# A two-layer graph network on one core: layer 1's leaky step moved from VectorE to GpSimd, and a mask made earlier

## The chip, the cores and the metric

The kernel runs on one core of one Trainium2 chip. The engines are TensorE (PE in the profile, PEld for its weight loads), VectorE (DVE), ScalarE (ACT), GpSimd (POOL) and SyncE (SP, which here only issues DMAs). Each engine works through its own instructions in the order in which they were written, and waits on semaphores for the others. The metric is the device time of one execution in microseconds.

## The reference

There are 16 graphs of 1024 nodes with 256 features, and an adjacency matrix of 0 and 1 for each. Layer 0 is attention with 8 heads over the neighbours, layer 1 attention with scores of its own and a leaky step. Each layer works on `h = relu(layernorm(x))` and adds its result to `x`.

```python
# layer 0: Q, K, V = proj(Wq, bq), proj(Wk, bk), proj(Wv, bv), 8 heads of 32
scores = einsum('bhnd,bhmd->bhnm', Q, K) * SCALE
scores = where(adj == 0, -inf, scores)
out    = einsum('bhnm,bhmd->bhnd', softmax(scores), V)
x      = x + einsum('bno,po->bnp', out, Wo) + bo
# layer 1, h = relu(layernorm(x))
e_k    = leaky_relu(einsum('bid,bjd->bij', h * a_k[:, 0], h), negative_slope=0.2)   # k = 0..3
scores = where(adj == 1, e_0, -9e15)      # and e_1, e_2, e_3 where adj is 2, 3, 4
x      = x + einsum('bij,bjd->bid', softmax(scores), h)
```

With an adjacency of 0 and 1 alone only `e_0` counts. The kernel checks this while it runs, and has a slow path (`layer_1_of_kinds`) for other values, which these inputs do not enter.

## The kernel before, in words

Work goes in tiles of 128 rows: 8 tiles (`NT`) to a graph, 128 in all. The main loop has 129 steps `s`, and in each step several tiles at different stages are worked on at once:

- `now` (`Attend`): layer 0's attention of tile `s`. For each head h, `scores` (L435, PE) writes 128x1024 scores into PSUM, `softmax_max` (L447, DVE) scales them, adds the mask and finds the row's extreme, `softmax_exp` (L455, ACT) takes the exponential one head later, and two heads later the result is transposed: heads 0, 1, 4 and 5 by DVE in blocks (L376) and four DMAs (L381), heads 2, 3, 6 and 7 by PE (L555) and copies on ACT (L556). `combine` (L490, PE) multiplies by the values.
- `was` (`Attend`): the end of tile `s - 1`: reciprocals of the sums (L471 and L472 on DVE, `wide` L474 on POOL, recT L484 on ACT), output matmul (L505), `residual` (L511, DVE), `norms` (statistics L188 and L189 on DVE, then `norm_of`, a chain of about 18 very small POOL instructions, L162 to L178), `normed` (L523, ACT). `gone` is the same tile one step later still: `turn_normed` (L530, PE) and the copy L534 (ACT).
- `nxt` (`Attend`): preparation of tile `s + 1`: `load_queries` (L402, a DMA from SP), `flag` (L427, ACT: reads the adjacency tile, leaves in `kinds_seen` whether it holds other values than 0 and 1) and `mask` (L415, POOL: writes -1e30 where the adjacency is 0, as bf16, over the same buffer `neg`). There are ten `neg` buffers, since layer 1 reads a mask again nine steps later. The adjacency tile (L406, a DMA from POOL) has one buffer.
- `edge` (`Edges`): layer 1 of tile `s - 9`, which is one graph and a tile later. `prepare` (L577, POOL) multiplies by a_0 into `ha`, `score` (L587, PE) makes the scores in two halves, `softmax_max` (L601, DVE) negates, masks and finds the row's extreme `top`, `leak` applies the leaky step, `softmax_exp` (L613, ACT) takes the exponential. In the next step the tile is `edge_was`: transposed in blocks by DVE, `gather` (L631, PE), `store` (L640, DVE, and a DMA).
- `piece`, `piece_was`, `piece_nxt`: the rows of the next graph are normalised and projected to queries, keys and values, one tile a step; keys are written to memory twice (L321, from SP and from POOL) and loaded as eight key tiles of a graph (`load_key`, L356, from POOL) around a change of graph, at the places in `KEY_STEPS`.

The order is written out by hand (`manual_schedule`): eight places h = 0 to 7 in a step, each with a list of calls. Before the change, `flag` and `mask` stand at h = 3 behind `load_queries`, `edge.softmax_max` at h = 2, `edge.leak` at h = 4, `edge_nxt.prepare` and the adjacency load at h = 4, `norms` at h = 5, `edge.softmax_exp` at h = 6, `was.normed` at h = 7. The exponential of head h - 1 stands at h, so that of head 7 comes first in the next step.

The tiles of the last graph (`last`, 8 of 128) go through layer 1 after the main loop, in a short loop of their own.

Of the kernel before, what the change touches and what calls it, by code (L numbers as in the profile page):

```python
# [8 lines left out]
F32 = mybir.dt.float32  # L9
# [5 lines left out]
ALU = mybir.AluOpType  # L15
AX = mybir.AxisListType

P = 128
# [5 lines left out]
SLOPE = 0.2  # L24
# [18 lines left out]
def gnn_kernel(  # L43
# [18 lines left out]
    nc = tc.nc  # L62
    B, N, D = x.shape
# [15 lines left out]
    work = ctx.enter_context(tc.tile_pool(name="work", bufs=2))  # L79
    ptp = ctx.enter_context(tc.tile_pool(name="ptp", bufs=7))  # L80
    dram = ctx.enter_context(tc.tile_pool(name="dram", bufs=2, space=bass.MemoryType.DRAM))
    small = ctx.enter_context(tc.tile_pool(name="small", bufs=4))
# [111 lines left out]
    class Piece:  # L194
# [5 lines left out]
        def __init__(self, b, first, n=1):  # L200
            self.b, self.first, self.n = b, first, n
            self.cols = slice(first * P, (first + n) * P)
            self.projected, self.halved, self.again, self.queries = [], [], [], []
            self.tags = ("xin", "h0", "hT", "halves", "hTm") if n == 1 else ("pT", "pT", "qt", "p", "blocks")
# [182 lines left out]
    h1s, h1Ts, x1ds, masks = {}, {}, {}, {}  # L387
# [171 lines left out]
    class Edges:  # L559


        def __init__(self, b, t, last=False):
            self.b, self.t = b, t
            self.rows = slice(t * P, (t + 1) * P)
            self.side = sides[t % 2 if last else 1]
            self.tags = {"sel": ("p", 4), "pT1": ("pT", 7)} if last else {}
            if last and t % 2:
                self.tags |= {"ha": ("hT", 1), "x1b": ("x1", 1)}
# [28 lines left out]

        def softmax_max(self):
            self.sel = self.buffer("sel", [P, N])
            top = small.tile([P, 1], F32, tag="top")  # L600
            nc.vector.tensor_tensor_reduce(  # L601
                out=self.sel, in0=self.e, in1=masks[self.b, self.t], scale=-1.0, scalar=3e38,
                op0=ALU.add, op1=ALU.min, accum_out=top,
            )
            self.nmx = small.tile([P, 1], F32, tag="nmx1")
            nc.vector.scalar_tensor_tensor(self.nmx, top, SLOPE, top, ALU.mult, ALU.min)

        def leak(self):
            nc.vector.scalar_tensor_tensor(self.sel, self.sel, SLOPE, self.sel, ALU.mult, ALU.min)

        def softmax_exp(self):
            self.total = small.tile([P, 1], F32, tag="total")
# [97 lines left out]
    def attend_of(s):  # L710
        return Attend(*divmod(s, NT)) if 0 <= s < B * NT else None
# [9 lines left out]
    with tc.manual_schedule():  # L721
        first = [Piece(0, 0, 4), Piece(0, 4, 4)]
        piece_was, piece_next = Piece(1, 0), piece_of(0)
        now, nxt = attend_of(0), attend_of(1)
# [36 lines left out]
        piece, edge, edge_was = piece_next, None, None  # L761
# [8 lines left out]
        for s in range(B * NT + 1):  # L770
            b, t = divmod(s, NT)

            def load_keys(h, end):
                if t == NT - 1 and b + 1 < B and 2 * h + end in KEY_STEPS:
                    load_key(b + 1, KEY_STEPS.index(2 * h + end))
                if t == 0 and 0 < b < B and 2 * (HEADS + h) + end in KEY_STEPS:
                    load_key(b, KEY_STEPS.index(2 * (HEADS + h) + end))

            nxt2, edge_nxt, piece_nxt = attend_of(s + 2), edges_of(s + 1), piece_of(s + 1)
            for h in range(HEADS):  # L780
                ending, eh = (now, h - 1) if h >= 1 else (was, HEADS - 1)
                turning, th = (now, h - 2) if h >= 2 else (was, HEADS + h - 2)

                load_keys(h, 0)


                if now:
                    now.scores(h)
                if h == 0 and piece_was:
                    piece_was.split()  # L790
                if h == 1 and piece_was:
                    piece_was.split()
                if h == 2 and edge:
                    edge.softmax_max()
                if h == 5:
                    if was:
                        was.residual()
                    norms(was, piece_nxt)
                if h == 6 and edge_was:
                    edge_was.gather(1)  # L800
                if h == 6 and piece_was:
                    piece_was.split()
                    piece_was.split()
                    piece_was.write_queries()
                if now:
                    now.softmax_max(h)
                if h == 6 and edge_was:
                    edge_was.store()
                if h == 4 and edge:
                    edge.leak()  # L810


                if ending:
                    ending.softmax_exp(eh)

                if h == 1 and gone:
                    gone.turned_normed()


                if h == 3:  # L820
                    if piece_was:
                        piece_was.project(1, 0)
                        piece_was.project(1, 1)
                    if was:
                        was.combine(1)
                    if piece_was:
                        piece_was.biased()
                    if was:
                        was.combined()
                if turning and th in BY_BLOCKS:  # L830
                    turning.turn_blocks(th)
                    turning.place_blocks(th)
                elif turning:
                    turning.turn(th, 0)
                    turning.turn(th, 1)


                if h == 0:
                    if piece_was:
                        piece_was.write_again()  # L840
                    if edge:
                        edge.score(0)
                    if gone:
                        gone.turn_normed()
                    if edge_was:
                        edge_was.turn_blocks()
                        edge_was.place_blocks()
                if h == 1:
                    if edge:
                        edge.score(1)  # L850
                    if was:
                        was.reciprocals()
                    if piece_nxt:
                        piece_nxt.load()
                    if piece_was:
                        piece_was.write_again()
                if h == 2:
                    if piece_was:
                        piece_was.values()
                    if was:  # L860
                        was.turn_reciprocals()
                        was.turned_reciprocals()
                        was.add_bias()
                    if edge_was:
                        edge_was.load_nodes()
                if h == 3:
                    if nxt:
                        nxt.load_queries()
                        nxt.flag()
                        nxt.mask()  # L870
                if h == 4:
                    if was:
                        was.output()
                    if piece:
                        piece.normed()
                    if edge_nxt:
                        edge_nxt.prepare()
                    if nxt2:
                        nxt2.load()
                if h == 5:  # L880
                    if edge_was:
                        edge_was.gather(0)
                    if piece:
                        piece.turn()
                    if piece_was:
                        piece_was.high()
                        piece_was.high()
                    if piece:
                        piece.turned()
                if h == 6:  # L890
                    if edge:
                        edge.softmax_exp()
                    if was:
                        was.keep()
                    if now:
                        now.load_nodes()
                    if piece:
                        piece.project(0, 0)
                        piece.project(0, 1)
                if h == 7:  # L900
                    if now:
                        now.combine(0)
                    if piece:
                        piece.high()
                        piece.high()
                    if was:
                        was.normed()
                load_keys(h, 1)
            gone, was, now, nxt = was, now, nxt, nxt2
            edge_was, edge = edge, edge_nxt  # L910
            piece_was, piece = piece, piece_nxt
# [6 lines left out]
        for i in range(1, len(tiles) + 2):  # L918
            edge = tiles[i] if i < len(tiles) else None
# [30 lines left out]
        top = small.tile([1, B + 1], F32, tag="tops", bufs=1)  # L950
# [41 lines left out]
```

## Time and profile before

| | |
|---|---|
| median of 3 runs | 3208.38 us (3190.67, 3208.38, 3210.05) |
| the profiled execution, first to last instruction | 3197.8 us |
| PE, DVE, ACT, POOL busy | 95%, 87%, 77%, 54% |
| granted clock of TensorE, mean | 0.985 |
| mask L415 on POOL, 128x1024 | 128 times, 3.647 us each |
| leaky step L609 on DVE, 128x1024 | 120 times, 1.216 us each (and 8 in the last graph) |

The profiled execution is one of its own; the span from its first to its last instruction is the only time that it shows, and it lies 10.6 us below the median of the runs. A row of the groups in the profile names line, engine, operation, the tiles written and read with their shapes, the count, then the busy time in us and the mean of one instruction in ns, and behind the second bar the idle time of the engine just before these instructions with what ended it. A row of the timeline names start and length in us, engine, line and operation; in square brackets stands how long the engine had been idle, and who released it.

### The profile page before, as it was taken

The page shows a single profiled execution, that of the slowest core. Times are in us where ns is not written, and L with a number is a line of the kernel's source. Part 1 is how long each engine was busy: PE and PEld are TensorE (multiplying, and loading weights), DVE is VectorE, ACT ScalarE, POOL GpSimd, SP SyncE. Part 2 cuts the span into 40 slices and gives each one's busy share as a digit, 9 for nine tenths or more (in the row PEclk, how much of TensorE's full clock was granted, in tenths as well). Part 3 has the DMA queues.
Part 4 walks back from the last instruction along what each step waited for, and adds up shares of the span by engine and source line. Part 5 has one row for each costly group of instructions (what it writes and reads, how often), then busy time and mean ns, then how long its engine had stood idle before and what let it go on. Part 6 is the DMA issues. An engine that isn't in the chain of part 4 may idle for free. (4 is left out here: it accounts for less than half of the span.)

```text
span 3197.8 us, 97634 instructions
## 1 busy us (share of the span) xinstructions
PE 3033.3 (95%) x36018; PEld 2216.3 (69%) x36018; DVE 2797.9 (87%) x5111; ACT 2454.3 (77%) x4829; POOL 1728.1 (54%) x3883
## 2 busy tenths in 40 slices
PE   5889999999999999999999999999999999998998
PEld 3667767777677777777677777777767677776663
DVE  3888989899898998989899998998989889898984
ACT  3887878788787877878788787887878778787761
POOL 2555555555555555555555655555555655555541
PEclk8999999999999999999999999999999999999999
DMA  6787788887888788788887878788887878888653
GB/s 226 219 244 233 227 273 233 259 240 231 270 240 272 226 253 249 226 277 234 252 238 230 275 233 273 230 254 263 235 272 226 269 228 232 267 240 249 194 161 91
DMA packets 747156, 762.90 MB, mean 239 GB/s; under 512 B 71281, under 2 KB 692209, under 8 KB 746673
## 3 DMA queue, kind: packets, MB, share of 16 engines
q1 hardware_dynamic: 678432, 542.34, 58.3%
q0 software_dynamic: 65040, 210.03, 20.3%
q8 instruction: 290, 4.75, 0.6%
q10 hardware_dynamic: 3200, 4.19, 0.4%
q14 instruction: 194, 1.58, 0.1%
HBM read 252.98 MB, written 167.77 MB: 132 GB/s over the span
## 5 line engine op out<-in xcount | busy, mean ns | idle before, releaser
L455 ACT ACTIVATE p<-p,nmx 128x1024 f32<-128x1024 f32 x1024 | 1178.5, 1151 | 249.6 <-DVE nmx L447 248.9
L447 DVE CUSTOM_DVE_ANT_0 p<-s,neg 128x1024 f32<-128x1024 f32 x1024 | 1233.3, 1205 | 92.0 <-issue 49.8
L435 PE MATMUL s<-k,qt 128*128 128x512 f32 x2048 | 795.0, 469 | 77.6 <-DMA qt<-qd 57.4
L415 POOL TENSOR_SCALAR neg<-adj 128x1024 bf16<-128x1024 int32 x128 | 466.8, 3647 | 411.8 <-ACT neg L427 411.8
L376 DVE STREAM_TRANSPOSE blocks<-p 128x1024 f32<-128x1024 f32 x520 | 642.3, 1235 | 11.3 <-ACT p L613 10.8
L556 ACT COPY pT<-trp 128x512 f32<-128x512 f32 x1024 | 543.6, 581 | 86.5 <-PE trp L555 78.6
L490 PE MATMUL acc<-pT,v 128*32 128x128 f32 x16384 | 525.1, 277 | 25.7 <-DMA pT<-blocks 24.3
L555 PE MATMUL trp<-ident,p 128*128 128x128 f32 x4096 | 534.7, 274 | 0.1
L555 PEld LDWEIGHTS trp<-ident,p 128*128 128x128 f32 x4096 | 480.9, 141 | 72.5 <-ACT pT L556 3.0
L490 PEld LDWEIGHTS acc<-pT,v 128*32 128x32 f32 x16384 | 450.7, 111 | 97.6 <-DVE ot L640 41.2
L631 PE MATMUL acc<-h,pT 128*32 128x256 f32 x8192 | 495.8, 383 | 4.0 <-DVE ot L640 3.2
L435 PEld LDWEIGHTS s<-k,qt 128*128 128x128 f32 x2048 | 330.3, 192 | 210.2 <-issue 122.6
L587 PE MATMUL s<-h1T,ha 128*128 128x512 f32 x992 | 471.1, 598 | 0.0
L631 PEld LDWEIGHTS acc<-h,pT 128*32 128x32 f32 x8192 | 242.6, 110 | 208.4 <-issue 58.7
L474 POOL COPY wide<-rec 128x256 f32<-128x256 f32 x128 | 50.8, 397 | 491.4 <-DVE rec L472 491.4
L321 POOL DMA_DIRECT2D kd<-halves x240 | 168.8, 703 | 228.7 <-DVE halves L294 216.2
L601 DVE CUSTOM_DVE_ANT_0 sel<-s,neg 128x1024 f32<-128x1024 f32 x120 | 147.0, 1225 | 126.4 <-PE s L587 126.4
L587 PEld LDWEIGHTS s<-h1T,ha 128*128 128x128 f32 x992 | 171.5, 193 | 124.1 <-issue 124.1
L455 ACT ACTIVATION_READ_ACCUMULATOR p<-p,nmx 128x1 f32 x1024 | 193.4, 189 | 0.0
L484 ACT COPY recT<-acc 128x256 f32<-128x256 f32 x128 | 47.8, 373 | 177.3 <-PE acc L480 177.3
L273 PEld LDWEIGHTS acc<-hT,wkT 128*128 128x128 f32 x960 | 120.8, 197 | 76.7 <-issue 47.3
L273 PE MATMUL acc<-hT,wkT 128*128 128x128 f32 x960 | 144.3, 295 | 27.3 <-DVE halves L294 26.1
(126 smaller groups left out, 4025.1 us busy)
## 6 DMA issues: line engine op xcount, KB each, us to landing
pT<-blocks SPq DMA_DIRECT2D x2560, 128.0 KB, 3.1
qt<-qd SPq DMA_DIRECT2D x128, 512.0 KB, 5.9
adj<-in_adj POOLq DMA_DIRECT2D x127, 512.0 KB, 5.5
qd<-halves SPq DMA_DIRECT2D x240, 256.0 KB, 4.6
k<-kd POOLq DMA_DIRECT2D x120, 512.0 KB, 6.8
kd<-halves POOLq DMA_DIRECT2D x240, 128.0 KB, 3.4
kd<-halves SPq DMA_DIRECT2D x240, 128.0 KB, 3.2
xb<-in_x POOLq DMA_DIRECT2D x128, 128.0 KB, 3.4
```

Source lines behind the costliest of these rows:

```text
L273: nc.tensor.matmul(ps, lhsT=wT[:, fc, oc * P : (oc + 1) * P], rhs=(self.hT, self.hTm)[which][:, fc, :], start=(fc == 0), stop=(fc == NC - 1),)
L321: queue.dma_start(out=kds[self.b][oc, :, :, twice, self.cols], in_=halves.rearrange("p (w n) -> p w n", w=2),)
L376: nc.vector.transpose(blocks.rearrange("p b j q -> p j b q"), p)
L415: nc.gpsimd.tensor_scalar(self.neg, self.adj, 0.0, MASKED, ALU.is_equal, ALU.mult)
L435: nc.tensor.matmul(self.ps[:, cols], lhsT=self.qt[:, h, :], rhs=keysets[self.b][h][:, cols], start=True, stop=True,)
L447: nc.vector.tensor_tensor_reduce(out=p, in0=sides[h in (3, 5, 7)], in1=self.neg, scale=-SCALE, scalar=FLOOR, op0=ALU.add, op1=ALU.min, acc ...
L455: nc.scalar.activation(p, p, AF.Exp, bias=nmx, scale=-1.0, accum_out=self.sums[:, h : h + 1])
L490: nc.tensor.matmul(sums_place[r * HD : (r + 1) * HD, g * P : (g + 1) * P], lhsT=vs[self.b][:, j, place_of(h) : place_of(h) + HD], rhs=self ...
L555: nc.tensor.transpose(tr[:, j, :], p[:, jj * P : (jj + 1) * P], ident)
L556: copy(pT[:, half * 4 : half * 4 + 4, :], tr)
L587: nc.tensor.matmul(self.e[:, cols], lhsT=self.ha[:, c, :], rhs=h1Ts[self.b][:, c, cols], start=(c == 0), stop=(c == NC - 1),)
L631: nc.tensor.matmul(sums_place[a * HD : (a + 1) * HD, :], lhsT=self.pT[:, j, a], rhs=h1s[self.b][:, j, :], start=(j == 0), stop=(j == NT - 1),)
```

## The change

The leaky step of layer 1's negated scores is `min(y, 0.2 y)`. Before, DVE does it in one instruction for a tile (and one small one for the row's extreme). After, `softmax_max` scales the scores by 0.2 as it negates them, so that the leaky step becomes `min(y, 5 y) = y + 4 min(y, 0)`; for all tiles but the last graph's, POOL computes it in four parts of 256 columns, each with a `tensor_scalar` (min with 0, times 4) into a small buffer `less` and an addition; the row's extreme is treated in the same way by two small POOL instructions. The last graph's tiles keep both instructions on DVE. `leak` goes from h = 4, behind the head's `softmax_max`, to the end of h = 3. `flag` and `mask` of the next tile go from h = 3 to the beginning of the list at h = 2.

```diff
-            self.b, self.t = b, t
+            self.b, self.t, self.last = b, t, last
...
         def softmax_max(self):
             self.sel = self.buffer("sel", [P, N])
-            top = small.tile([P, 1], F32, tag="top")
+            self.top = small.tile([P, 1], F32, tag="top")
             nc.vector.tensor_tensor_reduce(
-                out=self.sel, in0=self.e, in1=masks[self.b, self.t], scale=-1.0, scalar=3e38,
-                op0=ALU.add, op1=ALU.min, accum_out=top,
-            )
+                out=self.sel, in0=self.e, in1=masks[self.b, self.t], scale=-SLOPE, scalar=3e38,
+                op0=ALU.add, op1=ALU.min, accum_out=self.top,
+            )
+
+        def leak(self):
+            if self.last:
+                self.nmx = small.tile([P, 1], F32, tag="nmx1")
+                for to, y in ((self.nmx, self.top), (self.sel, self.sel)):
+                    nc.vector.scalar_tensor_tensor(to, y, 1 / SLOPE, y, ALU.mult, ALU.min)
+                return
+            g = nc.gpsimd
+            less = small.tile([P, 1], F32, tag="less1")
+            g.tensor_scalar(less, self.top, 0.0, 1 / SLOPE - 1, ALU.min, ALU.mult)
             self.nmx = small.tile([P, 1], F32, tag="nmx1")
-            nc.vector.scalar_tensor_tensor(self.nmx, top, SLOPE, top, ALU.mult, ALU.min)
-
-        def leak(self):
-            nc.vector.scalar_tensor_tensor(self.sel, self.sel, SLOPE, self.sel, ALU.mult, ALU.min)
+            g.tensor_tensor(self.nmx, self.top, less, ALU.add)
+            part = N // 4
+            for i in range(4):
+                sel = self.sel[:, i * part : (i + 1) * part]
+                less = work.tile([P, part], F32, tag="less", bufs=1)
+                g.tensor_scalar(less, sel, 0.0, 1 / SLOPE - 1, ALU.min, ALU.mult)
+                g.tensor_tensor(sel, sel, less, ALU.add)
...
-                if h == 4 and edge:
-                    edge.leak()
...
                 if h == 2:
+                    if nxt:
+                        nxt.flag()
+                        nxt.mask()
                     if piece_was:
                         piece_was.values()
...
                 if h == 3:
                     if nxt:
                         nxt.load_queries()
-                        nxt.flag()
-                        nxt.mask()
+                    if edge:
+                        edge.leak()
```

## The prediction

> **What bounds the kernel now.** I read first the page's busy times, then the waits, then one ordinary step as a timeline.
>
> ```profile
> PE 3033.3 (95%) x36018; PEld 2216.3 (69%) x36018; DVE 2797.9 (87%) x5111; ACT 2454.3 (77%) x4829; POOL 1728.1 (54%) x3883
> ```
>
> PE is nearly full and POOL is half idle. One ordinary step, mask to mask (length, then busy time of PE, PEld, DVE, ACT, POOL), shows PE without a gap:
>
> ```profile
> 1064.56:1087.78 23.22, 23.22 (x284) 17.13 (x283) 21.73 (x42) 19.22 (x39) 12.96 (x30) 1.00 0.81 230
> ```
>
> The starts of the mask (L415) give the step: 272.92 us to 2909.37 us is 110 steps of 24.0 us; ordinary ones take 23.2, the two around a change of graph about 26, and the last seven (to 3068.1) 22.7. What POOL's idle half consists of stands in the waits from 400 to 3000 us (total, times, longest):
>
> ```profile
> POOL wide L474 <- DVE rec L472: 419.1, 109, 9.7
> POOL neg L415 <- ACT neg L427: 327.9, 108, 4.4
> ...
> POOL ve L162 <- DVE mv L189: 23.4, 80, 4.5
> ACT h L523 <- POOL shift L178: 23.0, 25, 1.9
> ```
>
> POOL sits idle at two places: before `wide`, and before the mask, which waits for ACT's flag. Between the mask and the end of `norm_of` (L162 to L178) it runs without a pause, and the last line shows who stands behind it: ACT's L523 (`was.normed`), which already waits for POOL at times. ACT works in order, so behind L523 are queued exp(7), the copies of head 6, exp(0), and so on. Here is that path in an ordinary step (start, length, engine, line):
>
> ```profile
> 1069.22 0.59 POOL L406 DMA_DIRECT2D adj<-in_adj  x1
> ...
> 1070.00 0.22 POOL L162 TENSOR_SCALAR ve<-mv 128x2 f32<-128x2 f32 x1 [0.18 <-DVE mv L189]
> ...
> 1074.80 0.23 POOL L178 TENSOR_SCALAR shift<-shift 128x2 f32<-128x2 f32 x1
> ...
> 1075.06 0.60 ACT L523 ACTIVATE h<-x,shift,r 128x256 f32<-128x256 f32 x1
> ...
> 1079.65 1.04 PE L555 MATMUL trp<-ident,p 128*128 128x128 f32 x8
> ...
> 1079.86 0.37 ACT L534 COPY h1T<-acc 128x256 f32<-128x256 f32 x1
> ...
> 1080.29 1.08 ACT L556 COPY pT<-trp 128x512 f32<-128x512 f32 x2
> ...
> 1081.25 1.16 ACT L455 ACTIVATE p<-p,nmx 128x1024 f32<-128x1024 f32 x1
> ...
> 1082.45 1.23 DVE L601 CUSTOM_DVE_ANT_0 sel<-s,neg 128x1024 f32<-128x1024 f32 x1 [1.04 <-PE s L587]
> ...
> 1086.45 1.14 ACT L427 ACTIVATE neg<-adj,less_half 128x1024 bf16<-128x1024 int32 x1
> ...
> 1087.78 3.65 POOL L415 TENSOR_SCALAR neg<-adj 128x1024 bf16<-128x1024 int32 x1 [3.24 <-ACT neg L427]
> ...
> 1091.52 0.97 POOL L577 TENSOR_SCALAR ha<-h1T,a_t 128x128 f32<-128x128 f32 x2
> ...
> 1092.43 0.60 POOL L406 DMA_DIRECT2D adj<-in_adj  x1
> ```
>
> This is a loop: mask, `ha`, adj issue, norms on POOL; L523 to exp(1), exp(2) and flag on ACT; mask again. Its parts end to end are 3.74 + 0.91 + 0.66 + 5.03 + 0.03 + 6.31 + 0.37 + 1.15 + 1.33 = 19.5 us (the pieces are explained below). It has 3.7 us of slack in a 23.2 us step, so PE sets the step today.
>
> **What leaves DVE.** L609 (146.0 us over 120 tiles, 1.216 each) and L606 (0.363 each): 1.58 us a step. DVE is not what sets the step: L601 itself waits 1.04 us for PE in nearly every step. With PE full, lighter DVE work buys nothing in itself; the most it can give is the 0.37 us that the weight loads of L490 wait for the store's read of the sums (37.8 us in 103 waits on `ot`). The eight last tiles keep both operations on DVE in another order: nothing there. Scaling by 0.2 inside L601 is the same instruction.
>
> **The flag and mask move ahead.** No DMA belongs to them. On ACT the flag passes recT and exp(2) and lands after exp(1), where ACT idles some 1.5 us for PE (L484, 162.0 us in 109 waits): free. But a mask buffer is one of ten, and the flag of step s writes the buffer that L601 of the same step reads, so the flag now waits for L601. Both come together: with T the start of L523, exp(1) ends at T + 6.3; transposes of head 7 can start at T + 2.2, when the first copy of head 6 has emptied a buffer, L601 starts 2.80 later (1079.65 to 1082.45) and ends 1.23 after that, T + 6.3 too. On POOL the mask goes ahead of L419 and of the x1b issue L619, which ran in its wait until now; they are added to the loop: 0.67 and 0.61 (start to start).
>
> **The leak on POOL.** Ten instructions for each of 120 tiles. The two small ones: 0.22 and 0.20 as in `norm_of`. The four additions of 128x256 have an exact row, L419:
>
> ```profile
> L577 POOL TENSOR_SCALAR ha<-h1T,a_t 128x128 f32<-128x128 f32 x248 | 122.6, 502 | 18.6 <-PE s L587 8.0
> L419 POOL TENSOR_TENSOR xb<-xb,bo_t 128x256 f32<-128x256 f32 x128 | 110.5, 863 | 0.0
> ```
>
> 0.863 each. The four `tensor_scalar` (min, multiply) of 128x256 have none. From below: the plain copy L474 of 128x256, 0.40. From above by the nearest row, `ha`: 0.502 for 128 columns against 0.22 for two gives 2.2 ns a column, 0.78 for 256; it reads with a stride of 32, which these don't. From far above: the mask's 3.647 for 1024 gives 3.35 ns a column, 1.08. I take 0.60, midway between copy and `ha`. Dependent POOL instructions stand 0.08 apart in `norm_of`. Leak = 0.42 + 0.24 + 4 x (0.60 + 0.863 + 0.16) = 7.15 us; bounds 6.35 (at 0.40) and 9.07 (at 1.08).
>
> The Trainium skill ("GPSIMD Engine Reference", 3.1 "Elementwise") gives about 2.6 cycles an element at 1.2 GHz for a two-input operation and 1.8 at best otherwise, from which I estimate 0.55 and 0.38 us for 256 columns, a leak near 4.4 and a loop of 23.7: no change. The row L419, 0.86 and not 0.55, already speaks against using those rates alone. The same page's 4.1 advises VectorE for elementwise work, GpSimd being about twice as slow on two inputs; here the factor is about 6, 7.15 against 1.22, because one instruction becomes eight.
>
> **The loop after.** From mask to mask:
> - mask 3.74 (1087.78 to 1091.52), L419 0.67, L619 0.61, leak 7.15
> - `ha` to adj issue 0.91, adj issue to L162 0.66 (251.04 to 251.70, where L162 did not wait), norms 5.03 (1070.00 to 1075.03), to L523 0.03
> - ACT: L523 0.51 (1608.25 to 1608.76), exp(7) 1.14, copies 0.99, exp(0) 1.14, h1T 0.43, copies 0.96, exp(1) 1.14: 6.31. In the step shown L523 to exp(1) is 6.19 with waits inside but not behind it; run back to back it is this.
> - flag to mask 1.33 (1086.45 to 1087.78)
>
> Sum 26.5 us, 19.3 of it without the leak. It exceeds 23.2, so this loop takes over from PE. The other new wait, exp of `sel` (L613, with exp(6), L289 and L523 behind it on ACT) for the leak, costs nothing more: from the leak's end ACT needs 1.13 + 1.13 + 0.6 to reach L523, POOL 6.6. The adj load, issued 13.1 us after the mask's start, lands 5.5 later, 6 us ahead of the next flag. The x1b and xb loads also come in time.
>
> Around a change of graph POOL issues keys too. In the last step of a graph three (0.55 each) stand between mask and norms: 28.1. In the first step of a graph the key of head 7 is issued at head 4, so behind the leak: 5.02 + 0.6 + 7.15 = 12.8 after the mask, landing 6.8 later:
>
> ```profile
> k<-kd POOLq DMA_DIRECT2D x120, 512.0 KB, 6.8
> ```
>
> From scores(7) it is 6.5 us on PE to the transposes of the next head 7 (1073.17 to 1079.65), then 2.80 + 1.23 + 0.1 + 1.33 to the mask: 31.5 us for that step. Mean over eight: (6 x 26.5 + 28.1 + 31.5) / 8 = 27.3.
>
> Against 24.0: 110 x 3.3 = 363; the last seven 7 x (26.5 - 22.7) = 27; two leaks behind the last mask, 6. Together +396 on the span of 3197.8: 3594. The median of the runs is 10.6 above that span, so I say 3605 us.
>
> **Rivals.**
> - Milder: `tensor_scalar` costs what the copy does (0.40) and the late key is covered, as PE's five short waits for keys (4.4 us in all) suggest. Loop 25.6, with key issues 26.0: 110 x 2.0 + 7 x 3.0 + 5 = +246, 3455. Against it: two arithmetic operations are not a copy.
> - Heavier: 1.08 as the mask's slope says: loop 28.4, first and last steps 33.4 and 30.0, mean 29.2: 110 x 5.2 + 7 x 5.7 + 10 = +622, 3830. Against: the mask also converts int32 to bf16.
> - No change: a leak up to 24.0 - 19.3 = 4.7 us disappears in POOL's idle time and PE sets the step still: 3208. That leaves (4.7 - 0.66) / 4 = 1.0 us for a pair with its 0.16 of gaps, and so almost nothing for the `tensor_scalar`.
> - Faster: with a leak under 23.2 - 19.3 = 3.9 us the loop stays hidden, and DVE, 1.58 us a step lighter, frees the sums before L490 earlier: 120 x 0.37 = 44 less, 3165. It needs a pair of leak instructions in (3.9 - 0.66) / 4 - 0.16 = 0.65 us, when the addition alone has 0.86, and PE's full row leaves little to win.
>
> **How the numbers follow.** Forecast 0.62, milder 0.20, heavier 0.12, no change 0.03, faster 0.03. The range 3440 to 3770 takes in the milder case and the lower part of the heavier one. About 1% (32 us) can be told from no change: faster 0.03, same 0.03, slower 0.94.
>
> **What would show it.** Right: mask starts about 26.5 us apart; POOL at 75 to 80% without the long waits before `wide` and the mask; ACT's L523 waiting 4 to 5 us for L178 each step; PE at about 85%, its waits now on exp(7) and ACT copies. L621 shows the `tensor_scalar`. Wrong: mask starts still 23 us apart, or L523 seldom waiting; a step over 29 us would mean that POOL runs slower beside DVE than its rows say, or a wait I have not seen.

## The result, and the profile after

The changed kernel takes 3845.8 us (median of 4 runs, 3840.07 to 3855.04) against 3209.2 before: a ratio of 1.200, 95% interval 1.196 to 1.204. The profiled execution has a span of 3839.6 us. The direction and the mechanism were as forecast, the size was not: the forecast was 3605, with a range up to 3770.

First the busy times of the page, then two ordinary steps, mask to mask (length, busy time of PE, PEld, DVE, ACT, POOL, granted clock of PE, DMA share, GB/s).

```profile
PE 3235.0 (84%) x36018; PEld 2275.7 (59%) x36018; DVE 2649.0 (69%) x4871; ACT 2438.6 (64%) x4829; POOL 2657.7 (69%) x5083
```

```profile
1237.40:1266.96 29.56, 25.75 (x284) 17.86 (x283) 20.53 (x39) 19.01 (x39) 20.70 (x40) 0.94 0.63 184
1266.96:1294.86 27.90, 24.06 (x284) 17.03 (x284) 20.55 (x39) 19.04 (x39) 20.73 (x39) 1.00 0.65 194
```

No engine is full any more. Ordinary steps, those that are not at a change of graph, come mainly in two kinds, 27.9 and 29.6 us: of the 83 from the third graph on, 41 take 27.9 us and 29 about 29.6, and most of the others lie between. The longer kind shows a lower PE clock. The waits from 400 to 3700 us (total, times, longest) name the loop of the prediction:

```profile
ACT h L523 <- POOL shift L178: 451.1, 113, 5.2
POOL neg L415 <- ACT neg L427: 374.1, 111, 6.6
ACT sel L626 <- POOL sel L622: 346.5, 112, 5.4
...
PE acc L530 <- ACT h L523: 216.4, 99, 3.1
...
ACT neg L427 <- DVE top L601: 122.6, 113, 2.7
...
PE s L435 <- DMA k<-kd: 62.1, 22, 4.8
```

ACT waits for POOL's norms, POOL waits for ACT's flag, each in nearly every step: one chain that goes round. `L523 <- L178` was 23.0 us before (400 to 3000 us). The line of L427 and L601 is the new wait of the flag, which the prediction took to cost nothing. The third line, the exponential's wait for the leak, is long but lies beside the loop: in the turn below ACT has done this exponential and what follows it, and then still waits 3.75 us for L178. One turn of the loop, first on POOL (start, length, instruction):

```profile
1266.96 3.64 POOL L415 TENSOR_SCALAR neg<-adj 128x1024 bf16<-128x1024 int32 x1 [4.41 <-ACT neg L427]
1270.68 0.73 POOL L419 TENSOR_TENSOR xb<-xb,bo_t 128x256 f32<-128x256 f32 x1
1271.36 0.61 POOL L632 DMA_DIRECT2D x1b<-x1d  x1
1272.04 0.24 POOL L614 TENSOR_SCALAR less<-top 128x1 f32<-128x1 f32 x1
...
1272.62 1.09 POOL L621 TENSOR_SCALAR less<-sel 128x256 f32<-128x256 f32 x1
1273.80 0.73 POOL L622 TENSOR_TENSOR sel<-sel,less 128x256 f32<-128x256 f32 x1
...
1280.42 0.98 POOL L577 TENSOR_SCALAR ha<-h1T,a_t 128x128 f32<-128x128 f32 x2
1281.34 0.60 POOL L406 DMA_DIRECT2D adj<-in_adj  x1
1282.03 0.22 POOL L162 TENSOR_SCALAR ve<-mv 128x2 f32<-128x2 f32 x1
...
1286.85 0.23 POOL L178 TENSOR_SCALAR shift<-shift 128x2 f32<-128x2 f32 x1
```

and then from L523 back to the mask:

```profile
1287.11 0.60 ACT L523 ACTIVATE h<-x,shift,r 128x256 f32<-128x256 f32 x1 [3.75 <-POOL shift L178]
1287.62 1.14 ACT L455 ACTIVATE p<-p,nmx 128x1024 f32<-128x1024 f32 x1
...
1290.34 1.88 PE L587 MATMUL s<-h1T,ha 128*128 128x512 f32 x4
...
1292.26 1.23 DVE L601 CUSTOM_DVE_ANT_0 sel<-s,neg 128x1024 f32<-128x1024 f32 x1 [2.00 <-PE s L587]
...
1293.53 1.15 ACT L427 ACTIVATE neg<-adj,less_half 128x1024 bf16<-128x1024 int32 x1 [0.22 <-DVE top L601]
...
1294.86 3.65 POOL L415 TENSOR_SCALAR neg<-adj 128x1024 bf16<-128x1024 int32 x1 [2.72 <-ACT neg L427]
```

POOL runs without a pause from the mask to L178; the leak is 8.38 us of it (1272.04 to 1280.42). Its two operations of 128x256, and L419 beside them:

```profile
L621 POOL TENSOR_SCALAR less<-sel 128x256 f32<-128x256 f32 x480 | 514.8, 1073 | 40.1
...
L622 POOL TENSOR_TENSOR sel<-sel,less 128x256 f32<-128x256 f32 x480 | 352.2, 734 | 40.0
...
L419 POOL TENSOR_TENSOR xb<-xb,bo_t 128x256 f32<-128x256 f32 x128 | 93.4, 730 | 10.3 <-DMA xb<-in_x 0.2
```

### The profile page after: what moved, and what is told of

The parts are those of the page before. It is cut to its first block, busy times and chain, and to the rows that moved or that the text cites. A ratio compares the mean times of both kernels' runs of the same rounds, so it can differ in the third digit from the quotient of the medians.

```text
span 3839.6 us, 98599 instructions
## 1 busy us (share of the span) xinstructions
PE 3235.0 (84%) x36018; PEld 2275.7 (59%) x36018; DVE 2649.0 (69%) x4871; ACT 2438.6 (64%) x4829; POOL 2657.7 (69%) x5083
## 5 line engine op out<-in xcount | busy, mean ns | idle before, releaser
L447 DVE CUSTOM_DVE_ANT_0 p<-s,neg 128x1024 f32<-128x1024 f32 x1024 | 1236.6, 1208 | 190.4 <-PE s L435 178.6
L555 PE MATMUL trp<-ident,p 128*128 128x128 f32 x4096 | 588.7, 290 | 192.7 <-ACT p L455 124.6
L490 PE MATMUL acc<-pT,v 128*32 128x128 f32 x16384 | 554.2, 280 | 12.8 <-DMA pT<-blocks 6.2
L621 POOL TENSOR_SCALAR less<-sel 128x256 f32<-128x256 f32 x480 | 514.8, 1073 | 40.1
L490 PEld LDWEIGHTS acc<-pT,v 128*32 128x32 f32 x16384 | 475.4, 112 | 89.0 <-DVE ot L653 38.4
L587 PE MATMUL s<-h1T,ha 128*128 128x512 f32 x992 | 524.8, 657 | 0.5 <-ACT h1T L534 0.4
L523 ACT ACTIVATE h<-x,shift,r 128x256 f32<-128x256 f32 x128 | 76.7, 599 | 477.5 <-POOL shift L178 477.5
L622 POOL TENSOR_TENSOR sel<-sel,less 128x256 f32<-128x256 f32 x480 | 352.2, 734 | 40.0
L626 ACT ACTIVATE sel<-sel,nmx 128x1024 f32<-128x1024 f32 x120 | 138.2, 1151 | 375.1 <-POOL sel L622 375.1
L601 DVE CUSTOM_DVE_ANT_0 sel<-s,neg 128x1024 f32<-128x1024 f32 x120 | 147.0, 1225 | 310.2 <-PE s L587 310.2
L294 DVE SCALAR_TENSOR_TENSOR halves<-acc,bk_t,halves 128x128 fp32r<-128x128 f32 x240 | 83.2, 347 | 346.9 <-PE acc L530 237.7
L587 PEld LDWEIGHTS s<-h1T,ha 128*128 128x128 f32 x992 | 197.4, 221 | 150.5 <-issue 123.3
L474 POOL COPY wide<-rec 128x256 f32<-128x256 f32 x128 | 51.0, 398 | 303.4 <-DVE rec L472 289.0
```

Source lines behind the costliest of these rows:

```text
L447: nc.vector.tensor_tensor_reduce(out=p, in0=sides[h in (3, 5, 7)], in1=self.neg, scale=-SCALE, scalar=FLOOR, op0=ALU.add, op1=ALU.min, acc ...
L490: nc.tensor.matmul(sums_place[r * HD : (r + 1) * HD, g * P : (g + 1) * P], lhsT=vs[self.b][:, j, place_of(h) : place_of(h) + HD], rhs=self ...
L555: nc.tensor.transpose(tr[:, j, :], p[:, jj * P : (jj + 1) * P], ident)
L587: nc.tensor.matmul(self.e[:, cols], lhsT=self.ha[:, c, :], rhs=h1Ts[self.b][:, c, cols], start=(c == 0), stop=(c == NC - 1),)
L621: g.tensor_scalar(less, sel, 0.0, 1 / SLOPE - 1, ALU.min, ALU.mult)
L622: g.tensor_tensor(sel, sel, less, ALU.add)
```

## The experiments

Two theories stood against each other. One: a loop through POOL and ACT sets the step wherever it is longer than PE's 23.2 us. The other: POOL's work costs time as such, by contention or because the engine is slow. The loop also has parts that can be taken out one by one.

**The order alone (e1).** Only this edit, on the kernel before:

```diff
                 if h == 2:
+                    if nxt:
+                        nxt.flag()
+                        nxt.mask()
...
                 if h == 3:
                     if nxt:
                         nxt.load_queries()
-                        nxt.flag()
-                        nxt.mask()
```

> Only the flag and the mask move to h = 2; the leak stays on VectorE as before. Theory (a loop through GpSimd and ScalarE sets the step): without the leak the loop is 19.3 us, under PE's 23.2, so the time is that of the kernel before, 3209 us within 1%, and mask starts stay 23.2 us apart. Rival (the flag's new wait for L601 costs by itself): each step longer by up to 1 us, 3300 us.

Measured: 3266.7 us, ratio 1.019 (1.017 to 1.021). Ordinary steps are 23.37 us instead of 23.2, so the loop is hidden as expected; but the two steps around a change of graph rise from 25.8 and 25.9 us on average to 28.4 and 27.4. So the move is not free, and neither theory had the place right: the loss is mostly at the changes of graph. PE's waits show what is late there:

```profile
PEld s L435 <- DMA k<-kd: 34.4, 14, 3.5
PE s L435 <- DMA k<-kd: 33.4, 14, 3.3
```

The keys. On POOL the mask now stands ahead of two of the eight key issues of a graph, and they leave after it.

The move also puts POOL's `ha` beside DVE's leaky step L609, and both take longer there, 0.913 us instead of 0.502 and 1.435 instead of 1.216:

```profile
L577 POOL TENSOR_SCALAR ha<-h1T,a_t 128x128 f32<-128x128 f32 x248 | 224.5, 913 | 13.0 <-PE s L587 8.1
...
L609 DVE SCALAR_TENSOR_TENSOR sel<-sel 128x1024 f32<-128x1024 f32 x120 | 172.2, 1435 | 0.0
```

So work on the two engines can slow each other. In the changed kernel it does not show: L609 has left DVE, `ha` takes 0.498 us, and DVE's L447 and L601 take 1.208 and 1.225 against 1.205 and 1.225 before. By these rows contention does not explain its loss.

**The order alone, keys ahead again (e8), and its control (e9).** Three key loads one place earlier, on e1 and on the kernel before:

```diff
-    KEY_STEPS = (6, 9, 10, 13, 16, 20, 22, 24)
+    KEY_STEPS = (4, 9, 10, 13, 16, 19, 20, 24)
```

> The order alone (flag and mask at h = 2, leak on VectorE), with three of the eight key loads one place earlier (places 4, 19 and 20 in place of 6, 20 and 22), so that on GpSimd they stand ahead of the mask again. Theory (the order alone costs 57 us mainly because the key loads come behind the mask and the scores around a change of graph wait for them): the two steps at a change fall from 28.4 and 27.4 us to about 26, and the time to 3225 us; ordinary steps stay at 23.37. Rival (the loss is the flag's wait for L601 and exp(2) behind it, at the changes too): 3267 us.

> The kernel before with the same three key loads one place earlier, as the control for the run beside it. Theory (before the change the keys come in time): 3205 us, within 1%. Rival (keys are late there as well): 20 to 40 us less than before, 3175 us, and then a version faster than both kernels.

Measured: e8 3222.0 us, ratio 1.006 (1.004 to 1.009); e9 3202.0, ratio 1.000 (0.998 to 1.002). The waits for keys in e8:

```profile
PEld s L435 <- DMA k<-kd: 3.2, 5, 1.2
...
PE s L435 <- DMA k<-kd: 2.8, 5, 1.0
```

They are gone, and with them 45 of the 57 to 60 us. In the kernel before, the keys were in time, so there nothing is won. The 0.6% that is left was not taken apart; ordinary steps stay at 23.36 us, against 23.2.

**The leak alone (e2).** The changed kernel with flag and mask at h = 3, ahead of the leak:

```diff
                     if nxt:
                         nxt.load_queries()
+                        nxt.flag()
+                        nxt.mask()
                     if edge:
                         edge.leak()
```

> Only the leak moves to GpSimd, behind the mask at h = 3 where flag and mask were before. Theory: exp(2) and recT come back into the loop and the two POOL instructions L419 and x1b leave it: 3.74 + 8.38 + 0.91 + 0.66 + 5.03 + 0.03 on POOL, 10.3 from L523 to the mask: 29.1 us a step against 27.9 in the changed kernel, so about 3980 us. Rival (GpSimd's work as such costs the time, wherever the flag stands): 3846 us as the changed kernel.

Measured: 3941.2 us, ratio 1.229 (1.226 to 1.231). Ordinary steps are 28.9 to 30.4 us. The time is below the 3980 expected, but well above the rival's 3846: the same POOL work costs 95 us more when the flag stands behind exp(2): it is the way round that counts, and within the change the move of the flag wins part of the loss back.

**Half of the leak (e5).**

```diff
-            for i in range(4):
+            for i in range(2):
```

> The changed kernel with only two of the four parts of the leak, so half of the columns miss the leaky step. Theory (a loop that counts only where it is longer than PE's 23.2 us): the loop falls by 3.94 to 24.0 us in an ordinary step, with about 28.4 in the two around a change of graph a mean of 25.1, so 3340 us: more than three quarters of the loss gone with half of the work. Rival (GpSimd's work costs in proportion, by contention or otherwise): half way between the order alone (3267) and the changed kernel (3846), 3556 us.

Measured: 3295.0 us, ratio 1.029 (1.024 to 1.033). An ordinary step:

```profile
1130.25:1154.23 23.98, 23.63 (x284) 17.19 (x284) 20.33 (x39) 18.94 (x39) 17.16 (x35) 1.00 0.81 234
```

23.98 us, where 24.0 was expected: two parts less take 3.94 off the loop. The total lies below the 3340 expected, since the two steps around a change of graph took 25.8 and 28.0 us and not 28.4. Half of the leak costs only 28 us more than the order alone, the other half 551. That is a threshold, not a share.

**Flag and mask right behind `was.normed` (e7).** All of POOL's work stays; ACT's part of the loop shrinks to L523 and the flag.

```diff
                     if was:
                         was.normed()
+                    if nxt2:
+                        nxt2.flag()
+                        nxt2.mask()
```

(with flag and mask at h = 2 kept in step 0 only, an eleventh mask buffer, `KEPT = LAG + 2`, and two buffers shared to make room)

> The changed kernel with flag and mask of the tile after next right behind was.normed at h = 7, and eleven mask buffers (less shares its place with wide, ot with recT). All of GpSimd's work stays. Theory (a loop of GpSimd and ScalarE: now ScalarE's part of it shrinks from 7.7 us to 1.9): ordinary steps near 24.4 us, GpSimd busy almost throughout; with the changes of graph about 3350 us. Rival (GpSimd is slow beside the other engines, wherever the flag stands): 3700 us or more.

Measured: 3316.8 us, ratio 1.035 (1.031 to 1.039). An ordinary step:

```profile
1126.62:1150.91 24.29, 23.45 (x285) 17.04 (x284) 20.32 (x39) 18.96 (x39) 20.63 (x40) 1.00 0.80 223
```

POOL has the same 20.6 us of work as in the changed kernel, DVE and ACT too, and the step is 3.6 us shorter than the 27.9. Of the 637 us of the change, 529 go by placing two instructions elsewhere, with one mask buffer more (the next run has that buffer alone). It is still slower than before, now because POOL's chain from mask to L178 together with L523 and the flag, 24.3 us, is longer than PE's 23.2.

**Eleven masks (e3).**

```diff
-    KEPT = LAG + 1
+    KEPT = LAG + 2
```

(and the same two shared buffers)

> The changed kernel with eleven mask buffers in place of ten, so that the flag no longer waits for L601 (the buffer less shares its place with wide, ot with recT, to make room). Theory (steps of 29.6 us are those in which PE runs at half clock after its idle time, and the delay reaches the loop through L601 and the flag): every ordinary step near 27.6 us, in all about 120 us less, 3725 us. Rival (the slower clock delays the loop in another way, through the transposes of head 7, or only shows it): 3846 us.

Measured: 3714.2 us, ratio 1.159 (1.156 to 1.161). Three ordinary steps, all alike:

```profile
1228.36:1255.99 27.63, 25.13 (x286) 18.19 (x285) 20.60 (x39) 19.08 (x38) 20.72 (x40) 0.94 0.68 197
1255.99:1283.63 27.64, 25.07 (x286) 18.11 (x285) 20.60 (x39) 19.07 (x38) 20.73 (x39) 0.94 0.67 197
1283.63:1311.27 27.64, 25.26 (x287) 18.15 (x285) 20.61 (x41) 19.08 (x38) 20.73 (x39) 0.94 0.67 195
```

PE's clock still falls, in every step now (0.94), but the step stays at the loop's own length: with the flag free of L601, ACT runs on without a wait from L523 to the flag. That wait is worth 132 us in the changed kernel.

**PE kept busy (e6).** In the changed kernel, ahead of `turn_normed`:

```diff
                     if gone:
+                        if edge:
+                            for _ in range(14):
+                                nc.tensor.transpose(by_chunk(early)[:, 0, :], ident, ident)
                         gone.turn_normed()
```

> The changed kernel with 14 more 128x128 transposes of the identity on PE in each step, in the 2 us in which PE waits for L523 (their result is overwritten). Theory (PE's clock falls because PE sat idle there, and that makes half of the steps 29.6 us): the clock stays at 1.00 and ordinary steps are all 27.9 us, about 90 us less, 3755 us. Rival (the clock falls for another reason, or the added work itself is late): 3846 us or more, still with two kinds of steps.

Measured: 3793.0 us, ratio 1.184 (1.180 to 1.188). An ordinary step:

```profile
1281.99:1309.85 27.86, 25.61 (x298) 18.64 (x298) 20.57 (x39) 19.04 (x39) 20.67 (x39) 1.00 0.67 195
```

With PE's gap filled the clock stays at 1.00 in ordinary steps, and those of 29.6 us are gone. So idle time in PE brought the clock down. The time fell by 53 us and not by 90, since the second of the two steps around a change of graph rose from 31.6 to 33.3 us on average; why, was not tried. In six of these steps, read in the trace, the clock still fell, to a mean of 0.90 to 0.95 in the step.

**What a `tensor_scalar` costs (e4b).** The four parts in four forms, one execution, in which three parts compute something else than the leaky step:

```diff
+            g.tensor_scalar(less, parts[0], 0.0, None, ALU.min)
...
+            g.tensor_scalar(less, parts[1], 4.0, None, ALU.mult)
...
+            g.tensor_scalar(less, parts[2], 4.0, 0.0, ALU.mult, ALU.add)
...
+            g.tensor_scalar(less, parts[3], 0.0, 1 / SLOPE - 1, ALU.min, ALU.mult)
```

> The four parts of the leak use four forms of tensor_scalar on 128x256, each followed by the same addition: min alone, multiply alone, multiply and add, min and multiply (so three parts compute something else than the leaky step). Theory A (any tensor_scalar costs GpSimd some 3.3 ns a column, as the mask and L621 do): all four at 1.07 us. Theory B (min is what is dear; multiply and add cost what ha's row says): multiply forms at 0.6 to 0.78 us, min forms at 1.07. Theory C (each arithmetic step counts): one-step forms near 0.6, two-step forms near 1.07.

```profile
L627 POOL TENSOR_SCALAR less<-sel 128x256 f32<-128x256 f32 x120 | 129.0, 1075 | 10.5
...
L623 POOL TENSOR_SCALAR less<-sel 128x256 f32<-128x256 f32 x120 | 104.2, 868 | 10.9
L621 POOL TENSOR_SCALAR less<-sel 128x256 f32<-128x256 f32 x120 | 103.6, 863 | 0.0
...
L625 POOL TENSOR_SCALAR less<-sel 128x256 f32<-128x256 f32 x120 | 48.5, 404 | 10.5
```

In the order of the edit: min 0.863, multiply 0.868, multiply and add 0.404, min and multiply 1.075. None of the three theories has it: multiply and add together are less than half of a multiply alone, and cost what the plain copy L474 does.

## Why the prediction was right and wrong

**Right: what bounds the step.** The loop was added up from the rows of before, link by link, and with the leak's measured 8.38 in place of 7.15 it gives 27.7 us; the short steps are 27.9, those without the wait for L601 (e3) 27.6. Its tests held as well: half a leak 24.0, the flag moved forward 24.3 where about 24.4 was expected. Of the list of signs, PE at 84% came, and L523 waiting for L178 in nearly every step, though 3.75 us in an ordinary one and not 4 to 5. DVE's 1.58 us a step bought nothing.

Two signs did not come: POOL is busy 69% and not 75 to 80%, and its waits before `wide` and the mask have not gone (244.3 and 374.1 us). While ACT works through its 7.7 us of the loop POOL has little to do, so the loop itself asks for these waits. And steps over 29 us, the sign of "a wait I have not seen", did come; it was the wait for L601. Two small slips in the sums did not matter to the forecast: the terms of the loop add up to 26.44 us, not 26.5, and the estimate of 4.4 us for the leak leaves out the 0.16 us between instructions, with which it is 5.0.

**Wrong: the term of the `tensor_scalar`.** "I take 0.60, midway between copy and `ha`": it took 1.073. The row called "from far above", the mask, gave the right figure (1.08), though its pair is another and it converts types; why the figures agree was not tried. The prediction called `ha` the nearest row for its shape and its two operations, but its pair is multiply and add, the pair that e4b shows to be cheap, and so is no guide for min and multiply. The additions were cheaper, 0.734 for 0.863. Together the leak takes 8.38 us and not 7.15; 1.23 us over 120 tiles is 148 us.

**Wrong: "both come together".** The end of L601 was put at T + 6.3 beside the end of exp(1), and so at no cost. At full clock it is about right: L523 starts at 1287.11 and the flag at 1293.53, T + 6.4. But the sum took PE's pieces from steps in which PE was never idle. With the loop in charge PE waits some 2 us for L523, and in about half of the steps its clock falls just behind that, on the very matmuls that L601 waits for. The second half of a tile's scores, in the long kind of step:

```profile
1261.04 3.28 PE L587 MATMUL s<-h1T,ha 128*128 128x512 f32 x4
...
1264.35 1.23 DVE L601 CUSTOM_DVE_ANT_0 sel<-s,neg 128x1024 f32<-128x1024 f32 x1 [3.69 <-PE s L587]
...
1265.62 1.15 ACT L427 ACTIVATE neg<-adj,less_half 128x1024 bf16<-128x1024 int32 x1 [1.91 <-DVE top L601]
```

The four matmuls take 3.28 us instead of 1.88, and the flag starts at T + 8.1 (L523 at 1257.51). e3 prices the whole wait at 132 us, e6 shows that idle time is the cause of the slow clock.

**Missed: the keys at h = 3.** The prediction counted what the mask was moved past on ACT, named L419 and x1b on POOL, and added the time of three key issues to the last step of a graph. It did not ask when the two keys at the head of h = 3 land, which now leave behind the mask. With PE in charge that costs 45 us (e1 against e8); what it costs in the changed kernel was not measured. For the key of head 7 behind the leak, on the other hand, it asked too much: 31.5 us, which the measured leak makes 32.7, against 30.5 in e3.

So of the 246 us between the sum of 3594 and the span of 3839.6, the leak's size explains 148 and L601 132, together 34 too many; the overrated late key gives back 2.2 us at each of 14 changes of graph, 31.

**The rivals.** The heavier one (3830) had the right price and came near the total, partly by chance: it had neither the cheaper additions nor the clock. Milder, no change and faster are excluded by L621 and by the loop.

## What to carry to other kernels

Before moving work to an idle engine, follow that engine's chain round until it meets itself: the engine's idle time is usable only where its chain has slack, not where it waits for the next link. Here half of the moved work cost 28 us and the second half 551. Where a chain takes over from TensorE, see whether its clock falls behind the new gaps, as it did here in about half of the steps, and what hangs on the matmuls there. And price an elementwise instruction by a row with the same operations, not only the same shape.

## What the runs showed of the hardware

- PE's clock fell without any long pause. The longest single wait before the slow matmuls is 2.06 us; from 1255.00 to 1258.20 PE was busy 1.14 of 3.20 us, and the granted clock fell two microseconds later:

```profile
1255.00:1258.20 3.20, 1.14 (x4) 0.23 (x2) 1.44 (x3) 0.69 (x2) 2.54 (x11) 1.00 1.01 342
...
1261.00:1264.40 3.40, 3.40 (x8) 1.57 (x7) 0.05 (x1) 2.71 (x7) 1.46 (x3) 0.58 0.67 207
```

  From 1260.60 to 1263.80 the granted clock reads 0.50. The next step has the same gaps (PE busy 1.15 us from 1284.60 to 1287.80) and keeps its clock. The Trainium skill ("TensorE: Matmul & The Clock Gate", Part 1 "The HAM clock gate") says that the clock goes to half after an idle window of about 3.4 us, and that the window runs freely. The half rate and the chance from step to step agree with the runs; a full 3.4 us of idle time was not needed here.
- On GpSimd, multiply and add in one `tensor_scalar` of 128x256 takes 0.404 us, multiply alone 0.868, min and multiply 1.075.
- The same addition L419 takes 0.863 us before and 0.866 in e2, where it mostly follows a DMA issue on POOL, and 0.730 in the changed kernel and 0.728 in e1, where it follows the mask. What slows it was not tried.
- `ha` on POOL and the `scalar_tensor_tensor` L609 on DVE both take longer when they run side by side: 0.913 us for 0.502 and 1.435 for 1.216 in e1, 0.931 and 1.433 in e8.
